# Layer 0 of a four-layer image model: causal mask moved to VectorE, a 64-channel remainder computed by halves, decays spread by DMA

## The chip, the cores and the metric

The kernel is one program on one core of a Trainium2 chip. A core has a matrix engine (TensorE, PE in the profile, with its weight loads shown apart as PEld), a vector engine (VectorE, DVE), an activation engine (ScalarE, ACT), a general engine (GpSimd, POOL) and a queue engine (SyncE, SP) that issues most of the DMA transfers. Each engine executes its own list of instructions in order and waits on semaphores for the others. The metric is the device time of one launch in microseconds (us), lower is better. Before the change it is 15763.65 us, the median of three runs that lie between 15760.87 and 15764.36.

## The reference, cut to what matters

Four layers follow each other, each of the form x = x + layer(group_norm(x)), on 16 images of 192 channels of 32 x 32 pixels. Only layer 0 is touched. For each image it computes, with L = 1024 tokens (the pixels in order), 12 heads of 32 channels and an inner width of 384:

```python
h = _layernorm(seq, ln_w, ln_b)
x_in, z = jnp.split(h @ w_up + b_up, 2, axis=-1)
x_act = silu(causal_conv4(x_in))
q, k, v = x_act @ w_q, x_act @ w_k, x_in
i_pre, f_pre = gin @ w_i + b_i, gin @ w_f + b_f      # gin = concat(q, k, v)
# for each token: log_f = log_sigmoid(f);  m_new = max(log_f + m, i)
#   C = exp(log_f + m - m_new) * C + exp(i - m_new) * v k^T       (n likewise, with k)
#   h = C q / max(|n . q|, 1)
hn = per_head_norm(hs) * mh_w + mh_b
x1 = seq + ((hn + skip * x_act) * silu(z)) @ w_down + b_down      # 384 -> 192
y = conv3x3(x1 + silu(seq @ w_lin + b_lin)) + conv2_b             # then batch norm over all images
```

The recurrence over tokens is the part that the change is about. The batch norm at the end needs statistics over all 16 images, so the convolution's output goes to DRAM and is normalised by the code of the later layers.

## The kernel before, in words

`layer0` (lines 153 to 722) first loads the weights, and then loops over the 16 images with a hardware loop (`tc.For_i` on line 386). All instructions of one image are the loop's body. At its end the engines meet: each of them waits for the last work of every engine and for every DMA semaphore before it jumps back to the loop's start.

The recurrence is computed in 8 chunks of 128 tokens. Inside a chunk it is a product of matrices: for each head a 128 x 128 matrix of decays D, where D[s, t] = exp(a_t + (i_s - F_s)) for s up to t and zero for s after t, is multiplied by the scores k_s . q_t. Across chunks a state C (`cst`) and a normaliser n (`nst`) are carried, and q is scaled by a decay from the chunk's start (`isc`) before it meets them; the scaled q is `qs`.

The steps that the text follows are these.

- *Gates.* The gate values live with the heads on the partitions: `isc`, `wks`, `at`, `it` and their like (lines 430 to 485).
- *q's decays.* `qs` (lines 528 to 536): for each half of the tokens and each group g of four heads, a matmul with the constant `sel` spreads the four decays to 128 partitions in a PSUM bank, and VectorE multiplies q by them. That is 6 matmuls and 6 products for each image.
- *Scores.* `scores(n)`, n = 0 to 11 (lines 588 to 609), handles two (chunk, head group) pairs. It owns four PSUM banks S[0] to S[3], one for each head of the group. Columns 0 to 255 of a bank take the exponents of D, columns 256 to 511 the products of k and q. First four bfloat16 matmuls put the mask (0 or -1e30) into the four banks (line 595), then 16 matmuls add the exponents and 16 the products (line 600). ScalarE takes the exponential of the first half into an SBUF tile `d` (line 606), VectorE multiplies it by the second half (line 609).
- *A chunk's preparation and end.* `turned(c)` (lines 565 to 586) transposes v and k, and `finish(c)` (lines 611 to 678) multiplies D by v, adds the state's part, updates the state on VectorE and GpSimd, and normalises: ScalarE takes a square, TensorE a mean (lines 667 and 669), ScalarE a logarithm and an exponential (lines 670 and 671), VectorE the product and the affine part (lines 672 and 674), GpSimd the gate (line 678).
- *Fill.* `conv3(b)` (from line 348) is the 3 x 3 convolution of the image before, written as a generator: `fill(k)` issues its next k matmuls where TensorE would else wait. It reads `ypad`, the padded sum of the two branches of the image before. Channels 128 to 191 of `ypad` are held twice, on partitions 0 to 63 and, one column to the left, on partitions 64 to 127, so that one matmul covers two taps.
- *The order.* From `scores(0)` to the last `finish` the order is the program's own (`tc.manual_schedule()`); around it a scheduler orders the instructions. In that part the sequence for n = 0 to 11 is: scores, perhaps `turned`, and then either `finish` of a chunk (n = 2, 3, 5, 6, 8, 9, 11) or a fill of three matmuls (n = 0, 1, 4, 7, 10).
- *The two projections.* Lines 699 to 719 compute silu of the linear branch and the down projection for two groups of output channels, e = 0 (channels 0 to 127) and e = 1 (channels 128 to 191, twice side by side, so that the weights are 256 columns wide), for two halves hf of the tokens: 8 matmuls with `w_lin`, 12 with `w_down`, and six writes to `ypad` by VectorE on line 716. The sum with the input needs the normalised input on other partitions; four DMAs copy it to `xr`.

In all of this each float32 matmul is seen twice in the trace, as two passes.

Of the kernel before, what the change touches and what calls it, by code (L numbers as in the profile page):

```python
# [11 lines left out]
F32 = mybir.dt.float32  # L12
BF16 = mybir.dt.bfloat16
AF = mybir.ActivationFunctionType
ALU = mybir.AluOpType
AX = mybir.AxisListType
PSUM = bass.MemoryType.PSUM
DRAM = bass.MemoryType.DRAM

C, H, W = 192, 32, 32  # L20
L = H * W
HL = L // 2
P6 = 96
INNER, NH, DH = 384, 12, 32
CH = 128
# [6 lines left out]
def half(hf):  # L32
    return slice(hf * HL, (hf + 1) * HL)


def matmuls(nc, out, pairs):
    n = len(pairs)
    for i, (l, r) in enumerate(pairs):
        nc.tensor.matmul(out, lhsT=l, rhs=r, start=(i == 0), stop=(i == n - 1))
# [107 lines left out]
def rows(ap):  # L147

    return ap.rearrange("p (h w) -> p h w", w=W)
# [3 lines left out]
def layer0(tc, cx, NB, ydram, sdram):  # L153
    nc, I = cx.nc, cx.I
    with ExitStack() as ctx:
        wp = ctx.enter_context(tc.tile_pool(name="a_w", bufs=1))
        psp = ctx.enter_context(tc.tile_pool(name="a_ps", bufs=2, space=PSUM))
        pss = ctx.enter_context(tc.tile_pool(name="a_pss", bufs=1, space=PSUM))
        psn = ctx.enter_context(tc.tile_pool(name="a_psn", bufs=1, space=PSUM))
# [4 lines left out]
        def ps():  # L164

            turn[0] = (turn[0] + 1) % 6
            if turn[0] < 4:
                return pss.tile([128, HL], F32, tag="s%d" % turn[0], name="ps")
            return psp.tile([128, HL], F32, tag="ps", name="ps")
# [15 lines left out]

        w_down = wp.tile([128, 3, 256], F32, name="w_down")
        w_lin = wp.tile([P6, 2, 256], F32, name="w_lin")
        for t, nm, p in ((w_down, "w_down", 128), (w_lin, "w_lin", P6)):  # L190
            nc.sync.dma_start(t[:, :, 0:C], I[nm].rearrange("(k p) o -> p k o", p=p))
            nc.sync.dma_start(t[:, :, C:], I[nm][:, 128:C].rearrange("(k p) o -> p k o", p=p))
        w_c2 = wp.tile([128, 9, C], F32, name="w_c2")
        nc.sync.dma_start(w_c2, I["conv2_wT"][0:128])
        w_c2p = wp.tile([128, 2, 3, C], F32, name="w_c2p")
        for u in range(2):
            r = slice(64 * u, 64 * u + 64)
# [16 lines left out]
        b_down, b_lin, c2_b = vec3("b_down"), vec3("b_lin"), vec3("conv2_b")  # L214
# [12 lines left out]
        b_i, b_f = b_if  # L227
        conv_k = wp.tile([128, 3, 4], F32, name="conv_k")
        nc.sync.dma_start(conv_k, I["conv_k"].rearrange("(k p) t -> p k t", p=128))
        mask = wp.tile([128, 2 * CH], BF16, name="mask")  # L230
        identb = wp.tile([128, 128], BF16, name="identb")
        hmask = wp.tile([128, 4 * HW1], F32, name="hmask")
        nc.sync.dma_start(hmask, I["c_hmask"])
        nc.vector.tensor_copy(identb, cx.ident)

        blocks = wp.tile([128, 4, DH], F32, name="blocks")
        nc.vector.tensor_copy(blocks, hmask.rearrange("p (j d) -> p j d", d=HW1)[:, :, 0:DH])
# [18 lines left out]
        for u in range(2):  # L256
            for g in range(3):
                o = NH * u + 4 * g
# [33 lines left out]
        with tc.tile_pool(name="a_pre", bufs=1) as pre:  # L292
            m32 = pre.tile([128, CH], F32, name="m32")
            nc.sync.dma_start(m32, I["c_causal"])
            nc.vector.tensor_copy(
                mask.rearrange("p (i t) -> p i t", i=2),
                m32.unsqueeze(1).to_broadcast([128, 2, CH]),
# [88 lines left out]
        with tc.For_i(0, NB, 1) as b:  # L386
# [87 lines left out]
            isc = gp.tile([128, NCH, CH], F32, tag="e1", name="isc")  # L474
            nc.vector.tensor_add(isc, at3, mprev.unsqueeze(2).to_broadcast([128, NCH, CH]))
            nc.scalar.activation(isc, isc, AF.Exp)
            wks = gp.tile([128, NCH, CH], F32, tag="lf", name="wks")
            al = sm.tile([128, NCH], F32, tag="al", name="al")
            nc.vector.tensor_copy(al, at3[:, :, CH - 1])
# [40 lines left out]
            for c0 in range(0, NCH, 4):  # L520
# [3 lines left out]
                nc.vector.tensor_copy(  # L524
                    gtok[:, c0 : c0 + 4], p.rearrange("p (c r) -> p c r", c=4)[:, :, 0:NH]
                )

            qs = big.tile([128, 3, L], F32, tag="h", name="qs")
            for hf in range(2):
                for g in range(3):  # L530
                    p, r = ps(), slice(32 * g, 32 * g + 32)
                    nc.tensor.matmul(
                        p, lhsT=sel[r, g, :], rhs=isc.rearrange("p c t -> p (c t)")[r, half(hf)],
                        start=True, stop=True,
                    )
                    nc.vector.tensor_mul(qs[:, g, half(hf)], qT[:, g, half(hf)], p)

            for g in range(3):
                nc.scalar.activation(
# [48 lines left out]
            def scores(n):  # L588


                todo = [divmod(2 * n + i, 3) for i in range(2)]
                S = [pss.tile([128, HL], F32, tag="s%d" % j, name="s") for j in range(4)]
                two = slice(0, 2 * CH)
                for j in range(4):
                    nc.tensor.matmul(S[j][:, two], lhsT=identb, rhs=mask, start=True, stop=False)
                for l_, r_, o in ((itg, at, 0), (kT, qT, 2)):
                    for i, (c, g) in enumerate(todo):
                        cs = slice(c * CH, (c + 1) * CH)
                        for j, r in enumerate(blocks4):
                            nc.tensor.matmul(  # L600
                                S[j][:, (o + i) * CH : (o + i + 1) * CH], lhsT=l_[r, g, cs],
                                rhs=r_[r, cs] if o == 0 else r_[r, g, cs], start=False, stop=(o == 2 and i == 1),
                            )
                for j in range(4):
                    d = wk2.tile([128, 2 * CH], F32, tag="D", name="D", bufs=12)
                    nc.scalar.activation(d, S[j][:, two], AF.Exp)  # L606
                    for i, (c, g) in enumerate(todo):
                        D[c, g, j] = d[:, i * CH : (i + 1) * CH]
                    nc.vector.tensor_mul(d, d, S[j][:, 2 * CH :])  # L609

            def finish(c):

# [83 lines left out]
                pass  # L696


            xr = big.tile([128, 2, L], F32, tag="qT", name="xr")
            for r, e, q, a in (  # L700
                (slice(0, P6), 0, slice(0, P6), 0), (slice(P6, 128), 0, slice(0, 32), 1),
                (slice(0, 64), 1, slice(32, P6), 1), (slice(64, 128), 1, slice(32, P6), 1),
            ):
                nc.sync.dma_start(xr[r, e, :], xn[q, a, :])
            for e in range(2):
                for hf in range(2):
                    o = slice(e * 128, (e + 1) * 128)
                    pl = ps()
                    matmuls(nc, pl, [(w_lin[:, i, o], xn[:, i, half(hf)]) for i in range(2)])
                    lin = wk2.tile([128, HL], F32, tag="lin", name="lin")  # L710
                    nc.scalar.activation(lin, pl, AF.Silu, bias=b_lin[:, e : e + 1])
                    pd = ps()
                    matmuls(nc, pd, [(w_down[:, g, o], hT[:, g, half(hf)]) for g in range(3)])
                    nc.vector.tensor_add(lin, lin, xr[:, e, half(hf)])
                    for r, x in ((slice(0, 128), 1),) if e == 0 else ((slice(0, 64), 1), (slice(64, 128), 0)):
                        nc.vector.scalar_tensor_tensor(
                            ypad[r, e, 1 + 16 * hf : 17 + 16 * hf, x : x + W], rows(pd[r, :]),
                            b_down[r, e : e + 1], rows(lin[r, :]), op0=ALU.add, op1=ALU.add,
                        )

        for _ in conv3(NB - 1):
            pass
# [1245 lines left out]
```

## Time and profile before

| what | value |
|---|---|
| median of the runs | 15763.65 us |
| the profiled execution's own time | 15761.82 us |
| its span on the core | 15760.0 us |
| TensorE busy over the span | 12662.9 us (80%) |
| VectorE busy over the span | 12218.0 us (78%) |
| TensorE busy from 400 to 800 us, in layer 0 | 384.80 of 400 us |
| VectorE busy in the same stretch | 176.95 of 400 us |
| granted TensorE clock in the same stretch | 0.99 of full |
| restart of layer 0's loop on TensorE, two neighbours | 2477.89 and 2679.24 us |

The profiled execution took 1.82 us more than its span, and 1.83 us less than the median. Layer 0 lasts from the start to some 3328 us, where the last matmul of its convolution ends; one image takes a little over 201 us. A row of the profile names the line, the engine, the operation and the tiles; `busy` is the time in which an engine executes, and a releaser is what ended the idle time before. A busy TensorE is no TensorE at its peak, because matmuls overlap: their starts tell more than their durations.

### The profile page before, as it was taken

The page shows a single profiled execution, that of the slowest core. Times are in us where ns is not written, and L with a number is a line of the kernel's source. Part 1 is how long each engine was busy: PE and PEld are TensorE (multiplying, and loading weights), DVE is VectorE, ACT ScalarE, POOL GpSimd, SP SyncE. Part 2 cuts the span into 40 slices and gives each one's busy share as a digit, 9 for nine tenths or more (in the row PEclk, how much of TensorE's full clock was granted, in tenths as well). Part 3 has the DMA queues.
Part 4 walks back from the last instruction along what each step waited for, and adds up shares of the span by engine and source line. Part 5 has one row for each costly group of instructions (what it writes and reads, how often), then busy time and mean ns, then how long its engine had stood idle before and what let it go on. Part 6 is the DMA issues. An engine that isn't in the chain of part 4 may idle for free. (4 is left out here: it accounts for less than half of the span.)

```text
span 15760.0 us, 197355 instructions
## 1 busy us (share of the span) xinstructions
PE 12662.9 (80%) x72684; PEld 5062.6 (32%) x72684; DVE 12218.0 (78%) x10138; ACT 9273.8 (59%) x12098; POOL 9921.9 (63%) x5837
## 2 busy tenths in 40 slices
PE   8999999987777878778777777777787777878755
PEld 4555555542222222222222222222222222222212
DVE  4444444416898989989888898988989898988995
ACT  3333333325666666666666666666666666666664
POOL 0000000005687878787878787878878787878886
PEclk9999999998787878878788888888888887878766
DMA  1000000016787877778787878787877777777774
GB/s 26 15 15 15 15 14 15 15 47 168 193 202 196 198 199 192 207 185 209 180 209 182 210 186 209 185 210 186 204 193 196 194 200 192 198 201 188 203 181 114
DMA packets 858797, 2421.52 MB, mean 154 GB/s; under 512 B 117952, under 2 KB 237840, under 8 KB 850192
## 3 DMA queue, kind: packets, MB, share of 16 engines
q1 hardware_dynamic: 848592, 2407.09, 59.7%
q8 instruction: 583, 9.55, 0.3%
q10 hardware_dynamic: 9280, 2.08, 0.1%
q14 instruction: 342, 2.80, 0.1%
HBM read 2025.36 MB, written 366.67 MB: 152 GB/s over the span
## 5 line engine op out<-in xcount | busy, mean ns | idle before, releaser
L1829 POOL TENSOR_TENSOR hc<-h,cb 128x1024 f32<-128x1024 f32 x3072 | 7245.4, 2371 | 2057.6 <-DVE h L1817 1546.5
L1817 DVE TENSOR_TENSOR_SCAN h<-dA,xt 128x1024 f32<-128x1024 f32 x3072 | 6914.9, 2273 | 303.6 <-POOL hc L1829 295.9
L1808 DVE TENSOR_TENSOR xt<-xt,bb 128x1024 f32<-128x1024 f32 x3072 | 3632.9, 1227 | 929.7 <-ACT xt L1797 800.6
L1801 ACT ACTIVATE dA<-dl,A 128x1024 f32<-128x1024 f32 x3072 | 3506.3, 1146 | 778.6 <-DMA dl<-dld 670.2
L1859 PE MATMUL acc<-hc,sel 128*32 128x256 f32 x24576 | 2399.7, 471 | 1756.8 <-POOL hc L1829 1753.8
L766 PE MATMUL mm<-pad,dg 96*96 96x512 f32 (+1 forms) x5760 | 2964.3, 650 | 14.4 <-ACT pad L766 11.0
L1797 ACT COPY xt<-du 128x1024 f32<-128x1024 f32 x1536 | 1557.7, 1014 | 1387.9 <-DVE h L1817 1216.3
L1859 PEld LDWEIGHTS acc<-hc,sel 128*32 128x32 f32 x24576 | 560.6, 120 | 4094.9 <-POOL hc L1829 2956.9
L766 PEld LDWEIGHTS mm<-pad,dg 96*96 96x96 f32 (+1 forms) x5760 | 1022.0, 191 | 1517.1 <-issue 1400.8
L583 POOL TENSOR_TENSOR vw<-va,gtok 128x396 f32<-128x396 f32 x112 | 95.3, 851 | 1707.1 <-ACT va L575 1707.1
L766 PE MATMUL mm<-x,wgt 96*128 96x512 f32 (+1 forms) x1664 | 1055.2, 770 | 114.9 <-ACT z L766 42.8
L766 POOL TENSOR_TENSOR t<-x 96x512 f32<-96x512 f32 (+7 forms) x544 | 689.6, 1290 | 212.5 <-PE mm L766 199.9
L1850 PE MATMUL acc<-y,ident 128*128 128x512 f32 x576 | 444.1, 863 | 452.1 <-ACT y L1869 451.4
L678 POOL TENSOR_TENSOR x_in<-x_in,sz 128x384 f32<-128x384 f32 x128 | 116.8, 913 | 749.8 <-DVE x_in L674 674.0
L766 POOL TENSOR_TENSOR dlh<-dlh,e 128x512 f32<-128x512 f32 x384 | 488.6, 1272 | 157.4 <-ACT e L766 151.4
L766 PE MATMUL mm<-d,xT 128*96 128x256 f32 x2048 | 562.3, 412 | 19.2 <-ACT o L766 17.4
L766 POOL TENSOR_TENSOR duh<-dlh,xx 128x512 f32<-128x512 f32 x384 | 537.4, 1399 | 30.2
L766 PE MATMUL mm<-xd,dtw 12*128 12x512 f32 x768 | 532.8, 779 | 14.1 <-ACT dlh L766 14.1
L766 PEld LDWEIGHTS mm<-x,wgt 96*128 96x128 f32 (+1 forms) x1664 | 338.1, 223 | 633.5 <-issue 360.9
L374 PE MATMUL pc<-ypad,w_c 128*128 128x512 f32 (+1 forms) x1224 | 468.3, 631 | 89.3 <-PEq L386 46.1
L609 DVE TENSOR_TENSOR D<-D,s 128x256 f32<-128x256 f32 x768 | 271.0, 415 | 325.9 <-ACT D L606 325.9
L606 ACT ACTIVATE D<-s 128x256 f32<-128x256 f32 x768 | 232.7, 390 | 430.6 <-PE s L600 430.6
(314 smaller groups left out, 15277.6 us busy)
## 6 DMA issues: line engine op xcount, KB each, us to landing
dl<-dld SPq DMA_DIRECT2D x1536, 512.0 KB
du<-dud SPq DMA_DIRECT2D x1536, 512.0 KB
dld<-dlh SPq DMA_DIRECT2D x384, 256.0 KB
dud<-duh SPq DMA_DIRECT2D x384, 256.0 KB
bb<-xdr SPq DMA_DIRECT2D x128, 512.0 KB
cb<-xdr SPq DMA_DIRECT2D x128, 512.0 KB
dg<-dqd SPq DMA_DIRECT2D x288, 192.0 KB
xxd<-xg SPq DMA_DIRECT2D x16, 1536.0 KB
```

Of the source, the lines that this page charges most:

```text
L374: nc.tensor.matmul(p[r, :], lhsT=w_, rhs=v, start=(n == 0), stop=(n == 14))
L606: nc.scalar.activation(d, S[j][:, two], AF.Exp)
L609: nc.vector.tensor_mul(d, d, S[j][:, 2 * CH :])
L678: nc.gpsimd.tensor_mul(hT[:, :, cs], hT[:, :, cs], sz[:, :, cs])
L766: return f(out, *args, **kw)
L1797: self.nc.scalar.copy(self.xt[n], self.du[n])
L1801: self.nc.scalar.activation(self.dA[u % 3], self.dl[n % 2], AF.Exp, scale=self.A[:, blk, n : n + 1])
L1808: self.nc.vector.tensor_mul(self.xt[(n + 1 + blk) % 2], self.xt[n % 2], self.bb[blk])
L1817: nc.vector.tensor_tensor_scan(*views, 0.0, op0=ALU.mult, op1=ALU.add)
L1829: self.nc.gpsimd.tensor_mul(*views)
L1850: nc.tensor.matmul(acc, lhsT=self.cx.ident, rhs=self.y[:, g, half(pair)], start=True, stop=False)
L1859: nc.tensor.matmul(self.acc[rows4(q), q4(s)], lhsT=self.sel[:, m, :], rhs=self.hc[u % 3][:, q4(q)], start=False, stop=(s + m + blk == 3),)
```

## The change

Three parts of layer 0 are computed in other ways. What follows after the loop stays as it was, instruction for instruction, on every engine.

First, the mask. The four mask matmuls at the start of `scores` go away, and with them the bfloat16 identity. The first exponent matmul into each bank now starts the bank. The exponential of a masked entry can then be large, so VectorE limits D to 2 as it multiplies by the scores, and a second VectorE product multiplies by a mask of ones and zeros. The pool of `d` tiles grows from 12 to 14.

Second, q's decays. `isc` is written to DRAM, read back with each row repeated over 32 partitions by three DMAs, and multiplied by q with three GpSimd products. The six matmuls and six VectorE products go away.

Third, the projections. Channels 128 to 191 are computed once, with the two halves of the tokens side by side: partitions 0 to 63 take half 0, partitions 64 to 127 half 1. That makes three output tiles in place of four; the third has ten matmuls of 64 output rows. Two DMAs inside SBUF then copy each half of these channels to where the convolution's second copy lies. The weights lose their doubled columns and two load DMAs.

```diff
-            nc.sync.dma_start(t[:, :, 0:C], I[nm].rearrange("(k p) o -> p k o", p=p))
-            nc.sync.dma_start(t[:, :, C:], I[nm][:, 128:C].rearrange("(k p) o -> p k o", p=p))
+            nc.sync.dma_start(t, I[nm].rearrange("(k p) o -> p k o", p=p))
...
+            nc.vector.tensor_scalar(m32, m32, -1.0, 1.0, op0=ALU.max, op1=ALU.add)
...
             nc.scalar.activation(isc, isc, AF.Exp)
+            nc.sync.dma_start(iscd, isc[0:NH].rearrange("p c t -> p (c t)"))
+            qs = big.tile([128, 3, L], F32, tag="h", name="qs")
+            for g in range(3):
+                nc.sync.dma_start(
+                    qs[:, g, :], iscd[4 * g : 4 * g + 4].unsqueeze(1).to_broadcast([4, DH, L])
+                )
...
-            qs = big.tile([128, 3, L], F32, tag="h", name="qs")
-            for hf in range(2):
-                for g in range(3):
-                    p, r = ps(), slice(32 * g, 32 * g + 32)
-                    nc.tensor.matmul(
-                        p, lhsT=sel[r, g, :], rhs=isc.rearrange("p c t -> p (c t)")[r, half(hf)],
-                        start=True, stop=True,
-                    )
-                    nc.vector.tensor_mul(qs[:, g, half(hf)], qT[:, g, half(hf)], p)
+            for g in range(3):
+                nc.gpsimd.tensor_mul(qs[:, g, :], qs[:, g, :], qT[:, g, :])
...
-                for j in range(4):
-                    nc.tensor.matmul(S[j][:, two], lhsT=identb, rhs=mask, start=True, stop=False)
...
-                                rhs=r_[r, cs] if o == 0 else r_[r, g, cs], start=False, stop=(o == 2 and i == 1),
+                                rhs=r_[r, cs] if o == 0 else r_[r, g, cs],
+                                start=(o == 0 and i == 0), stop=(o == 2 and i == 1),
...
-                    d = wk2.tile([128, 2 * CH], F32, tag="D", name="D", bufs=12)
+                    d = wk2.tile([128, 2 * CH], F32, tag="D", name="D", bufs=14)
...
-                    nc.vector.tensor_mul(d, d, S[j][:, 2 * CH :])
+                    nc.vector.scalar_tensor_tensor(
+                        d, d, 2.0, S[j][:, 2 * CH :], op0=ALU.min, op1=ALU.mult
+                    )
+                    nc.vector.tensor_mul(d, d, mask)
...
-            for e in range(2):
-                for hf in range(2):
-                    o = slice(e * 128, (e + 1) * 128)
-                    pl = ps()
-                    matmuls(nc, pl, [(w_lin[:, i, o], xn[:, i, half(hf)]) for i in range(2)])
-                    lin = wk2.tile([128, HL], F32, tag="lin", name="lin")
-                    nc.scalar.activation(lin, pl, AF.Silu, bias=b_lin[:, e : e + 1])
-                    pd = ps()
-                    matmuls(nc, pd, [(w_down[:, g, o], hT[:, g, half(hf)]) for g in range(3)])
...
+            for n in range(3):
+                e = n // 2
+                parts = [(n, slice(0, 128), slice(0, 128))] if n < 2 else [
+                    (0, slice(128, C), lower), (1, slice(128, C), upper)
+                ]
+                pl, pd = ps(), ps()
+                for p, w_, v, k in ((pl, w_lin, xn, 2), (pd, w_down, hT, 3)):
+                    for i in range(k):
+                        for hf, o, r in parts:
+                            nc.tensor.matmul(
+                                p[r, :], lhsT=w_[:, i, o], rhs=v[:, i, half(hf)], start=(i == 0), stop=(i == k - 1)
+                            )
...
+            nc.sync.dma_start(ypad[upper, 1, 1:17, 0:W], ypad[lower, 1, 1:17, 1 : 1 + W])
+            nc.sync.dma_start(ypad[lower, 1, 17:33, 1 : 1 + W], ypad[upper, 1, 17:33, 0:W])
```

In the new order of instructions the DMAs of the decays stand on SP's queue after the load of the next image and ahead of the convolution's stores; the three GpSimd products are that engine's first work in an image; and the two copies inside SBUF are the last entries of SP's queue before the loop's end. On TensorE the projections come as: `w_lin` of tile 0, the last `finish`, `w_lin` of tiles 1 and 2, the first `w_down` matmul of tile 2, then `w_down` of tile 0, tile 1, and the other five of tile 2.

## The prediction

> **What bounds the kernel now.** I first read the stretches of layer 0, which lasts some 3.3 ms of 15.8; the rest is left as it was, instruction for instruction. The columns are length and busy time of PE, PEld, DVE, ACT and POOL.
>
> ```profile
> core 0: us, PE busy (x) PEld busy (x) DVE busy (x) ACT busy (x) POOL busy (x), PEclk, DMA share, GB/s
> 464.00:665.40 201.40, 193.80 (x1812) 105.52 (x1812) 88.76 (x179) 78.11 (x150) 18.20 (x30) 0.99 0.05 14
> ```
>
> One image: TensorE works 193.8 of 201.4 us, VectorE 88.8, GpSimd 18, the DMA engines 5%. So TensorE sets the pace, and work moved to the others is free unless it makes TensorE wait. Who waits for whom on TensorE over layer 0 (us in total, times, longest) says where the other 7.6 us go:
>
> ```profile
> PE pc L374 <- PEq L386: 46.1, 15, 3.2
> PE pc L374 <- ACT yo L377: 39.0, 32, 1.4
> PE s L595 <- DVE qs L536: 15.8, 48, 0.3
> PE ps L39 <- POOL x_in L678: 13.5, 16, 1.0
> ```
>
> 3.1 us an image at the loop's end (L386), 2.4 for the convolution's bank, 1.0 where the first mask matmuls wait for the qs products, 0.8 for the last chunk. Then the timeline of TensorE before the first scores:
>
> ```profile
> 2559.06 1.99 PE L532 MATMUL ps<-isc,sel 32*128 32x512 f32 x12
> 2560.98 1.12 PE L374 MATMUL pc<-ypad,w_c2p 64*128 64x512 f32 x2
> 2562.16 0.27 PE L595 MATMUL s<-mask,identb 128*128 128x256 bf16 x1
> 2562.75 0.27 PE L595 MATMUL s<-mask,identb 128*128 128x256 bf16 x1 [0.33 <-DVE qs L536]
> ...
> 2564.15 0.73 PE L600 MATMUL s<-at,itg 32*128 32x128 f32 x16
> ```
>
> and an ordinary step, where four masks take 0.53 us from start to start (2570.62 to 2571.15):
>
> ```profile
> 2570.62 0.60 PE L595 MATMUL s<-mask,identb 128*128 128x256 bf16 x4
> 2571.15 0.73 PE L600 MATMUL s<-at,itg 32*128 32x128 f32 x16
> ```
>
> Last the loop's end, VectorE's last write and TensorE's restart, and then the stretches before and after the restart, where the first number after POOL's is the granted clock:
>
> ```profile
> 2676.23 1.51 DVE L716 SCALAR_TENSOR_TENSOR ypad<-ps,v_b_down,lin 64x512 f32<-64x512 f32 x2 [1.23 <-PE ps L39]
> 2679.24 3.57 PE L374 MATMUL pc<-ypad,w_c 128*128 128x512 f32 x4 [3.05 <-PEq L386]
> ```
>
> ```profile
> 2676.00:2679.20 3.20, 0.19 (x1) 0.00 (x0) 1.62 (x3) 0.16 (x1) 0.00 (x0) 0.98 0.00 0
> 2679.20:2682.60 3.40, 3.35 (x4) 1.45 (x5) 2.63 (x7) 1.12 (x1) 0.00 (x0) 0.51 0.00 0
> ```
>
> The restart comes 1.50 us after VectorE's end at 2677.74, and the next 3.4 us run at clock 0.51.
>
> [...] restarts at 464.07 and 2880.61 lie 12 images apart, 201.38 us each, which is 59.0 such windows. [...] here the small store to `sdram`, issued at 2658.46, released ScalarE at 2660.60, 2.14 us. [...] no row of layer 0 shows pieces of 128 B.
>
> **The change, for one image; 16 of them.**
>
> *Masks, n = 1 to 11.* Eleven times 0.53 us go, some 0.1 of each perhaps needed again for the switch of tile shape: 11 x 0.50 = -5.5.
>
> *The start.* From 2559.06 to 2564.15 are 5.09 us; only the convolution's 1.1 stays: -4.0. Nothing else is late there: the last copy of k (L499) ended at 2558.52, and scores(0) would start near 2560.2.
>
> *Decays by DMA.* `isc` is ready at 2743.26 in the next image, 20.5 us ahead of its first scores. The store takes some 2.4 us, the reads 1.5 MB: the 768 KB of the next image kept the engines 47% busy for 6 us, 2.8 us of full work, so 5.6 here plus 2.4 of latency. They land near 2754. SP has no store to make between (the next is at 2767). GpSimd's three products at 2.37 us (the 128x1024 row of line 1829) are in order with q's last copy at 2756.8 and end by 2762; `vw`, queued behind them, is wanted at 2763 or later, and `qs` itself only by the second `finish`, over 20 us later. Cost 0; without that cover the products' 7 us would be seen. The six VectorE products (3.7 us) were hidden but for the wait counted above.
>
> *The VectorE products.* A bank is now released after a limited product from PSUM (0.415 us, as L609) and, for all but the first, the pairs before it. [...] a pair about 0.80 with the overlap of neighbours. 48 x 0.42 = 20 us more for VectorE, which had over 110 idle. But where a `finish` comes right before, VectorE starts D late: in step n = 4 TensorE ends the norm's matmuls at P = 2591.51, and D starts at 2594.23, P + 2.72. The fourth bank comes free at P + 2.72 + 3 x 0.80 + 0.42 = P + 5.54. Without masks TensorE wants it at P + 1.10 (scores) + 1.10 (turned) + 2.87 (fill) + 0.1 = P + 5.17: a wait of 0.4. Step 7 is like it; step 10, with a shorter `turned` (5.22 from mask to mask before, 4.69 now), waits 0.75. In the other steps D starts 1.6 after scores and the bank is free by 4.4, wanted at 4.8 or later; D itself is read a step later. Sum +1.5, from 0 (if the pair costs 0.65) to +3.
>
> *Projections.* Eight passes fewer at full width, but the last chunk's values come at 2670.77 by the chain through ScalarE (with four table loads), VectorE and GpSimd, which doesn't move. Behind them stood 12 passes of 0.43; now 6 of 0.43 and at most 10 of 0.23 (the convolution's 64-row form does 12 in 2.73): 4.9 for 5.2, -0.3. What is saved ahead of 2670.77 becomes idle time, 3.6 to 4.2 us, and may halve the clock for the passes behind: 0 to +1.7, taken as +0.5.
>
> *The copies inside SBUF.* They are issued after VectorE's last writes, and every engine waits for their semaphores at the loop's end; nothing hides them. A copy has 64 x 16 pieces of 128 B, 64 for each of 16 engines. From issue to landing a store of 64 rows took 2.4 us (the two stores of `yo`: 2658.88, the second held until 2661.26). For pieces I have the three 4-byte loads of `tq` after layer 0: 3456 pieces, about 2.9 us of DMA work on 16 engines, 14 ns a piece, so 0.9 us. Together +3.3. Low end +2.1 (the small store); high end, at four times the price of a piece (64 x 0.056 + 2.4 = 6.0) and with a part of the first copy still in line, +7.
>
> *Start of the launch.* Two loads fewer on SP, which idles from 3.84 to 6.66 behind one of them: 0 to -4 once, taken as -2.
>
> Sum: -5.5 - 4.0 + 1.5 - 0.3 + 0.5 + 3.3 = -4.5 us an image, 196.9, which is 57.7 clock windows. The loop restarts in step with these windows, because a restart that comes late in one has less slow time ahead of it. The nearest whole number is 58, 197.97 us, and I take that: -3.4 x 16 - 2 = -57 us. In the profiled execution 15760.0 + 1.8 - 57 = 15705; the median is 1.8 above that execution, so 15707, taken as 15705.
>
> **The rivals.**
>
> *Ledger without the lock* (0.28): -4.5 x 16 - 2 gives 15690; with the low ends of waits, clock and copies -7.7 x 16 - 2, 15639.
>
> *Gain swallowed* (0.15): waits for the fourth bank at their high end and the copies at +5, -1.3 an image, or a lock at 59 windows: 15740 to 15764. For it: both unknown costs lie on the path. Against: it needs both.
>
> *Copies as a bottleneck* (0.09), slower: [...] The sum turns at +7.8 for the loop's end, and passes +0.2% at +9.8: with 128 pieces on each engine in line and 2.4 us of latency, that is 58 ns a piece, four times my figure. At 100 ns it is +15.2, giving 15880. Against: the 4-byte loads.
>
> *Decays late* (under 0.03): the second `finish` would wait for `qs`; needs a delay of over 20 us.
>
> **How the numbers follow.** Likeliest, 58 windows or near it: 0.45, its own range 15690 to 15725. With the rivals 0.28, 0.15, 0.09 and 0.03 the range 15640 to 15770 leaves out some 0.17. About 0.2% (32 us) is what a measurement of this kernel can tell from no change; faster by more: 0.76, within: 0.15, slower: 0.09.
>
> **What would show it.** Lines 595 and 532 are gone; scores(0) starts 5 us sooner after the `wks` transposes; short waits of TensorE on the D rows in steps 4, 7 and 10; TensorE's gap at the loop's end grows from 3.1 to some 6 us, with a DMA as releaser; the restart's period is near 198. I am wrong if the copies land over 8 us after VectorE's end, if D's waits appear in every step, or if the layers after layer 0 change by more than 20 us.

## The result: no gain, and the profile after

The changed kernel takes 15772.4 us (median of 20 runs) against 15763.1 for the kernel before: a ratio of 1.0004, 95% interval 0.9998 to 1.0010. The forecast was 15705. The 57 us expected are not there.

All three parts did what they say, and the work did leave TensorE. The stretches of one image of layer 0 in the changed kernel (length, busy time of PE, PEld, DVE, ACT and POOL, granted clock, DMA share, GB/s):

```profile
core 0: us, PE busy (x) PEld busy (x) DVE busy (x) ACT busy (x) POOL busy (x), PEclk, DMA share, GB/s
461.10:662.50 201.40, 187.34 (x1752) 100.98 (x1752) 109.19 (x218) 77.40 (x149) 26.82 (x33) 0.97 0.08 22
```

TensorE is busy for 187.3 us instead of 193.8, VectorE for 109.2 instead of 88.8, and the image still takes 201.4. The saved time has turned into waiting and slow clock. Who TensorE waits for over layer 0 (us in total, times, longest):

```profile
PE pc L375 <- PEq L387: 100.4, 15, 6.9
PE ps L718 <- POOL x_in L681: 62.5, 16, 4.0
PE pc L375 <- ACT yo L378: 40.1, 33, 1.4
PE s L598 <- DVE D L609: 14.8, 48, 0.3
```

The loop's end went from 46.1 to 100.4 us and the wait for the last chunk of `hT` from 13.5 to 62.5. The convolution's wait (40.1) is the old one, and the last line stands where the wait for `qs` stood.

An image can be cut at three points of TensorE's timeline: its first exponent matmul (`scores(0)`), the end of the last norm matmul (the `dsel` row of the last `finish`), and its last row. In us, for the image that restarts at 2477.89 before and at 2475.32 after:

```
                                        before   after   difference
restart to scores(0)                     86.26   82.49     -3.77
scores(0) to the last norm matmul        95.48   93.79     -1.69
last norm matmul to TensorE's last row   16.56   18.37     +1.81
TensorE's last row to the restart         3.05    6.63     +3.58
sum                                     201.35  201.28     -0.07
```

The first piece went as forecast. On TensorE's timeline `scores(0)` follows the `wks` transposes and the convolution's one row, with no broadcast products and no masks between:

```profile
2555.74 1.09 PE L531 MATMUL ps<-ident,wks 128*128 128x128 f32 x8
2556.76 1.12 PE L375 MATMUL pc<-ypad,w_c2p 64*128 64x512 f32 x2
2557.81 0.73 PE L598 MATMUL s<-at,itg 32*128 32x128 f32 x16
```

The second piece lost most of its gain behind steps 4, 7 and 10: VectorE's products of these steps hold the banks that the scores of steps 5, 8 and 11 want. The products of step 4 and the scores of step 5, from the same timeline, rows of TensorE, VectorE and GpSimd (start, duration):

```profile
2589.02 0.78 PE L598 MATMUL s<-at,itg 32*128 32x128 f32 x6
2590.11 0.59 PE L598 MATMUL s<-at,itg 32*128 32x128 f32 x9 [0.31 <-DVE D L609]
...
2590.55 0.71 PE L598 MATMUL s<-qT,kT 32*128 32x128 f32 x13
2591.19 0.86 PE L622 MATMUL nd<-D,va 128*32 128x128 f32 x24
...
2586.58 0.41 DVE L609 SCALAR_TENSOR_TENSOR D<-D,s 128x256 f32<-128x256 f32 x1
2587.03 0.91 DVE L612 TENSOR_TENSOR D<-D,mask 128x256 f32<-128x256 f32 x1
2587.86 0.41 DVE L609 SCALAR_TENSOR_TENSOR D<-D,s 128x256 f32<-128x256 f32 x1
2588.30 0.62 DVE L612 TENSOR_TENSOR D<-D,mask 128x256 f32<-128x256 f32 x1
...
2589.64 0.41 DVE L609 SCALAR_TENSOR_TENSOR D<-D,s 128x256 f32<-128x256 f32 x1
...
2586.76 0.91 POOL L681 TENSOR_TENSOR x_in<-x_in,sz 128x384 f32<-128x384 f32 x1 [4.04 <-DVE x_in L677]
2587.62 1.03 POOL L583 TENSOR_TENSOR vw<-va,gtok 128x396 f32<-128x396 f32 x1
```

The scores of step 5 take from 2589.02 to 2591.19, 2.17 us, where an undisturbed step takes 1.1. So the step loses 1.07 us, of which the list above counts only the 0.31 of idle time. The fourth bank comes free only after the last limited product (L609, end 2590.05), and three mask products (L612) stand ahead of it. The first two of these ran beside products of two inputs on GpSimd and took 0.91 and 0.62 us. Over all of layer 0, the 462 mask products that overlap no GpSimd instruction take 0.42 to 0.43 us; the median is 0.63 for the 128 that overlap L583 alone, and 0.92 for the 96 that overlap L681.

The third piece, the tail. First the windows around the last chunk's arrival, then TensorE's timeline:

```profile
2659.30:2662.70 3.40, 0.00 (x0) 0.00 (x0) 2.83 (x7) 2.83 (x4) 0.90 (x1) 1.00 0.00 0
2662.70:2666.10 3.40, 3.39 (x5) 1.50 (x6) 0.50 (x1) 0.00 (x0) 0.00 (x0) 0.61 0.02 5
2666.10:2669.60 3.50, 3.50 (x12) 0.75 (x10) 0.75 (x1) 0.00 (x0) 0.00 (x0) 0.90 0.00 0
```

```profile
2655.02 3.80 PE L718 MATMUL ps<-x_in,w_down 128*64 128x512 f32 x8
2662.71 7.26 PE L718 MATMUL ps<-x_in,w_down 128*128 128x512 f32 x16 [3.89 <-POOL x_in L681]
2676.60 2.05 PE L375 MATMUL pc<-ypad,w_c 128*128 128x512 f32 x2 [6.63 <-PEq L387]
```

TensorE stands idle for 3.89 us, and the 16 passes behind the wait run at clock 0.61 and 0.90. They take 7.26 us from the first start to the last end; the same 16 passes take 5.46 at full clock, in the run below that moves the Silu rows. The clock's record has one stretch of half clock here, 3.41 us long, from 0.71 us after their start. The fourth piece is the gap of 6.63 us in the last row. VectorE had its last write at 2671.54; the restart is 5.06 us later, where it was 1.50.

### The profile page after: what moved, and what is told of

Same layout as the page of the kernel before. It is cut to its first block, busy times and chain, and to the rows that moved or that the text cites. A ratio compares the mean times of both kernels' runs of the same rounds, so it can differ in the third digit from the quotient of the medians.

```text
span 15778.2 us, 196250 instructions
## 1 busy us (share of the span) xinstructions
PE 12591.2 (80%) x71724; PEld 4999.5 (32%) x71724; DVE 12539.0 (79%) x10762; ACT 9264.7 (59%) x12082; POOL 10055.9 (64%) x5885
## 5 line engine op out<-in xcount | busy, mean ns | idle before, releaser
L536 POOL TENSOR_TENSOR qs<-qs,qT 128x1024 f32<-128x1024 f32 x48 | 112.9, 2353 | 1534.3 <-DMA qs<-iscd 1518.4
L779 POOL TENSOR_TENSOR t<-x 96x512 f32<-96x512 f32 (+7 forms) x544 | 689.3, 1288 | 228.5 <-PE mm L779 208.7
L375 PE MATMUL pc<-ypad,w_c 128*128 128x512 f32 (+1 forms) x1224 | 471.0, 633 | 147.1 <-PEq L387 100.4
L681 POOL TENSOR_TENSOR x_in<-x_in,sz 128x384 f32<-128x384 f32 x128 | 116.7, 912 | 692.4 <-DVE x_in L677 692.4
L612 DVE TENSOR_TENSOR D<-D,mask 128x256 f32<-128x256 f32 x768 | 427.4, 556 | 26.3
```

The source lines that it names most:

```text
L375: nc.tensor.matmul(p[r, :], lhsT=w_, rhs=v, start=(n == 0), stop=(n == 14))
L612: nc.vector.tensor_mul(d, d, mask)
L681: nc.gpsimd.tensor_mul(hT[:, :, cs], hT[:, :, cs], sz[:, :, cs])
L779: return f(out, *args, **kw)
```

## The experiments

Theory A is the table: terms that add up, with three sinks (bank waits, the idle tail with its slow clock, the copies at the loop's end). Theory B, a rival, is that the period can only be a whole number of clock windows of 3.413 us, so that a gain below the next step is lost whatever it came from; both kernels have periods of 59.0 such windows. The windows are read from the clock's record in the two profiles: the 17 stretches of half clock up to 3300 us before, and the 32 after, are all 3.413 or 6.827 us long, and within a profile start whole multiples of 3.4133 us apart, to within 0.002. Theory C is, in each run, that the suspected cause isn't one. Times given as differences are the ratio, less one, times 15763. Periods are the mean distance of restarts of the loop in the profile.

**The third part alone.** The kernel before, with the loads and the projections of the changed one.

> The kernel before with the projections' part of the change alone (last 64 channels by halves side by side, two copies inside SBUF at the loop's end, two loads fewer); masks and decays as before. Theory A (the ledger with the terms as the trace of after shows them: loop end +3.6 us, cold clock in the passes behind the last chunk about +1.8): the loop's period grows from 201.4 to 206 to 207 us, total about +80 us over before, near 15845. Theory B (the period keeps to whole clock windows of 3.413 us): 204.8 or 208.2 us, +55 or +109 us. Theory C (this part costs next to nothing, the gain was lost elsewhere): period 201.4 to 202, total within 15 us of before.

Ratio 1.0083 (1.0070 to 1.0097), +131 us; periods mostly 208.2, mean 208.7. C falls: this part costs 7 us an image. Against before the tail grew by 2.81 us and the gap at the loop's end by 3.75. A was 2 us too low: the 16 passes behind the last chunk took some 8.2 us here and not 7.26, with half clock for 6.83 us and not 3.41. B's 208.2, or 61 windows, is met by twelve images of fourteen (207.9 to 208.3). The other two last 212.0 and 212.1; in each the clock is at half for 10.24 us more, about the start of the second piece.

**The other two parts without the third.** The changed kernel with the loads and projections of before, `D` in 13 buffers.

> The changed kernel with the projections of before (full width, no copies inside SBUF): masks as a product and decays by DMA alone; 13 buffers for D in place of 14, for room. Theory A: start -3.8 and masks with their waits -1.7 us an image, so a period of about 196 us and -85 us against before, near 15678. Theory B (whole windows): 197.9 us (58 windows, -55 us) or 194.5 (57, -109 us). Theory C (the gain is lost in the bank waits and not at the loop's end): period 201 and no gain.

Ratio 0.9949 (0.9935 to 0.9962), -80 us; mean period 195.86. A's sum is met. B as it is stated is not: single periods lie between 194.9 and 196.9, 57.1 to 57.7 windows.

**The decays alone**, in the kernel before: `iscd`, the store, the three loads and the GpSimd products replace the matmuls of L532 and the products of L536.

> The kernel before with the decays' part alone (decays by DMA, product with q on GpSimd; masks and projections as before). Only three of six broadcast products of TensorE a head group go, so the first mask matmuls stay. Theory A (removed work comes off the path): 2.0 to 2.4 us off before the first scores, no wait for qs; period 199.0 to 199.5, or less by up to 1.6 if restarts come warm. Theory B (whole windows): 201.4 (no gain) or 198.0. Theory C (the DMA part makes something late): slower than before.

Ratio 0.9968 (0.9956 to 0.9980), -50 us; period 197.93. The expectation counted the removed matmuls wrongly (all six go), so the gain that A names, 2.0 to 2.4 us, was too small: the first piece shrinks by 3.4, from 86.26 to 82.87, of which the matmuls are 1.99 and the wait for `qs` 1.0. A's period holds only with its allowance for warmer restarts, and 197.93 is also B's 198.0, so this run doesn't tell the two apart. Nothing came late.

**The masks alone**, in the kernel before, `D` in 13 buffers.

> The kernel before with the masks' part alone (product on VectorE; decays and projections as before; 13 buffers for D). Theory A: 5.8 us of mask matmuls in 11 steps and some 2 in the first step go, bank waits of 3.4 us and about 0.7 of switching come: -3 to -4 us an image, period 197.5 to 198.5. Theory B (whole windows): 198.0 or 201.4. Theory C (VectorE's extra work delays more than the banks): no gain, 201.

Ratio 0.9989 (0.9981 to 0.9997), -17 us; mean period 200.4. Nearer to C than to A. TensorE's timeline at the first scores shows why:

```profile
2550.16 2.39 PE L598 MATMUL s<-at,itg 32*128 32x128 f32 x15
2552.29 0.28 PE L598 MATMUL s<-qT,kT 32*128 32x128 f32 x3
```

Fifteen passes take 2.39 us where 16 take 0.73 in the full change: VectorE's six `qs` products, still there, end at 2551.90, and the scores take over their PSUM banks. In the kernel before, the masks' matmuls stood in this place and did the waiting (the 0.33 us for `qs` at 2562.75). Then TensorE waits another 1.2 us for `yo`, and in ten images of fourteen the clock is at half for 3.4 or 6.8 us about here; in this image the next six passes take 5.05 us and not 2.84, at clock 0.50. So the masks' part gains more beside the decays' part: alone they shorten the period by 1.0 and 3.4 us, together by 5.5.

**The order of VectorE's products.** In the changed kernel:

```diff
-                    nc.vector.tensor_mul(d, d, mask)
+                    ds.append(d)
+                for d in ds:
+                    nc.vector.tensor_mul(d, d, mask)
```

> The changed kernel with another order on VectorE: the four limited products of a step first, which free the four banks, and then the four mask products. Nothing is left out. Theory A: the waits for banks in steps 4, 7 and 10 (3.4 us an image) go almost whole, period 198.0 to 198.5 us, -45 to -55 us against after, near 15720. Theory B (whole windows): 198.0 us, or no change at all if the 3.4 us are not quite saved. Theory C (the waits in these steps come from something other than the mask product ahead of the bank's release): waits and time stay as in after.

Ratio 0.9971 (0.9961 to 0.9981), -46 us against before; period 197.96. The wait for banks is gone from the list, and the second piece is 90.36 us instead of 93.79. The scores of step 5 and the products of step 4 in this kernel, TensorE and then VectorE:

```profile
2546.94 0.73 PE L598 MATMUL s<-at,itg 32*128 32x128 f32 x16
2547.49 0.60 PE L598 MATMUL s<-qT,kT 32*128 32x128 f32 x13
...
2544.50 1.40 DVE L610 SCALAR_TENSOR_TENSOR D<-D,s 128x256 f32<-128x256 f32 x4
2545.82 1.85 DVE L615 TENSOR_TENSOR D<-D,mask 128x256 f32<-128x256 f32 x4
```

All four banks are free at 2545.9, before TensorE wants the first. The mask products' place ahead of the banks' release is shown as the cause of the waits, 3.43 us an image. As 3.43 us is also one window to within 0.02, the run says nothing on B.

**Half a window more work.** In the changed kernel four matmuls of zeros are added to the sums of the first scores step:

```diff
+                    for j in range(4 if n == 0 and o == 2 else 0):
+                        nc.tensor.matmul(
+                            S[j][:, two], lhsT=w_c2[:, j, 0:128],
+                            rhs=zero.to_broadcast([128, 2 * CH]), start=False, stop=False,
+                        )
```

> The changed kernel with four more matmuls of 128x256 (two passes each, with a moving operand of zeros, so the sums are unchanged) in the first scores step of each image, where TensorE never waits: 1.7 us an image, half a clock window. Theory A (no lock): period 203.1 us, +27 us against after, near 15800. Theory B (the period keeps to whole windows): 201.4 and no change, or 204.8 and +55 us.

Ratio 1.0046 (1.0032 to 1.0059), +72 us against before, +66 against the changed kernel; period 204.82, that is 60.0 windows. The added passes take 2.01 us, and the period grew by 3.40. So B holds here. In the mean over the images the second piece, which holds the added passes, grew by 2.1. The rest is slow clock: the passes behind the last chunk took 8.34 us and not 7.26, with half clock for two windows (6.83 us) and not one, and the restart's piece and the gap grew by 0.2 together.

**Without the copies.** The two DMAs inside SBUF are removed, which leaves that part of the work out.

> The changed kernel without the two copies inside SBUF at the loop's end, so one row of the last 64 channels' halves lacks in ypad: this leaves out part of the work. Theory A (the copies cost what the trace shows between VectorE's end and the restart, 3.6 us): period 197.8 us, -57 us against after. Theory B (whole windows): 58 windows, 198.0 us, -55 us, or 57 (194.6) if a shorter gap at the loop's end also leaves less slow time. Theory C (the barrier at the loop's end costs this in any case, copies or not): no change.

Ratio 0.9961 (0.9947 to 0.9974), -61 us against before; mean period 197.90. TensorE's last row to the restart is 3.06 us, as before the change. C falls: it is the copies and not the barrier, 3.57 us an image. The rounding is loose: three periods of 197.4 and one of 199.5, in turn, make 232 windows in four images.

**Both good parts, with the order.** The second run's kernel with the reordered products.

> Masks and decays of the change, projections of before, and the four limited products of a step ahead of the four mask products. Nothing is left out. Theory A (costs simply add): the run without the reordering had a mean period of 195.85 us; less the bank waits of 3.4 us gives 192.4, -145 us against before, near 15615. Theory B (whole windows when the slow clock after the restart can take up the difference): without slow clock the period would be some 191.5 us, 56.1 windows; it is 56 windows (191.2), 57 (194.6), or swings between images as without the reordering, where some restarts came warm. Theory C (nothing more to be had): as without the reordering, 15680.

Ratio 0.9904 (0.9889 to 0.9919), -151 us. Mean period 191.9, single ones 191.6 and 192.4: A's 192.4 and 15615 against 15617.6 measured. It is not a whole number of windows (56.2), though B had named such swings between images as a third way. The second piece is 90.36 again.

**Its tail by hand, and with the clock kept up.** Two kernels made from the last one: one with the order of the projections written out, and one that adds two matmuls of zeros at the end of an image:

```diff
+                fl = ps()
+                for i, w in enumerate((HL, 128)):
+                    nc.tensor.matmul(
+                        fl[:, 0:w], lhsT=w_c2[:, i, 0:128], rhs=zero.to_broadcast([128, w]),
+                        start=(i == 0), stop=(i == 1),
+                    )
+                nc.scalar.copy(zero, fl[:, 0:1])
```

> As the run before it in this list, with the tail written out by hand: all four w_lin products, then the w_down products of both tiles of the first half, then of the second half with the single write of the first 128 channels last; ScalarE's Silu rows come after the last finish and not between its Ln and Exp. Nothing is left out. Theory A (TensorE bounds the tail): its gap of 0.8 us before the last chunk goes, and one write of 0.6 us less stands behind its last row: -1.4 us an image, about -22 us. Theory B: a whole window or none, -55 us or 0. Theory C: the chain through ScalarE does not bound this tail and no gain appears.

> As the run before it in this list, with two matmuls more at the end of an image (128x512 and 128x128 on a moving operand of zeros, 1.1 us, result copied on ScalarE into the zero it came from), so that TensorE idles about 2 us and not 3 at the loop's end. Theory A (the slow clock after the restart is only a cost): the restart comes warm in more images, -1.0 to -1.6 us an image, -16 to -26 us. Theory B (the slow clock is also what holds the period at whole windows): the period is no longer a whole number of windows and takes the value without slow clock, near 190 us. Theory C (2 us of idle time are enough to halve the clock): no change, or +0.3 us an image if the copy comes after VectorE's end.

0.9926 (0.9912 to 0.9939) and 0.9916 (0.9902 to 0.9931); mean periods 193.40 and 193.35. The first is a miss: the Silu rows still stood between Ln and Exp on ScalarE, and the `w_lin` pair that used to run ahead of the last `finish` was now behind it, so TensorE waited 28.1 us in all for `h` there (2.5 in the changed kernel). The second missed A's gain of 1.0 to 1.6 us and B's period near 190, and is what its theory C had allowed for. But it shows what the slow clock does. All its restarts come at full clock (four passes in 1.96 us, where those of before take 3.57), and its 14 periods lie between 193.34 and 193.39, 56.65 windows. Without the fill they swung from 192.97 to 193.72. So in these two kernels the slow time after a restart is what moves the period about, and where it is gone the period is constant and on no whole window. There was no gain: the restart's piece shrank by 0.41 us, and the last two pieces grew by 0.36, since the fill's copy on ScalarE ended 0.5 us after VectorE and held up the barrier.

**Silu behind the last finish.** In the changed kernel the tail is written out with TensorE's rows in the same order, and ScalarE's Silu rows after Ln and Exp (`lin_mm` and `down_mm` issue the matmuls of a tile; `last` is the list of those of the 64-row tile):

```diff
+                lin_mm(0)
                 finish(ready)
...
+                for n in range(3):
+                    if n:
+                        lin_mm(n)
...
+                    nc.scalar.activation(lin, pls[n], AF.Silu, bias=b_lin[:, e : e + 1])
...
+                down_mm(2, last[:1])
+                down_mm(0, [(i, tiles[0][1][0]) for i in range(3)])
+                down_mm(1, [(i, tiles[1][1][0]) for i in range(3)])
+                down_mm(2, last[1:])
```

> The changed kernel with its tail written out: TensorE's rows in the same order as in the changed kernel, but ScalarE's three Silu rows behind the last finish's Ln and Exp and not between them. Nothing is left out. Theory A (the last chunk of hT comes late by the Silu rows and their table loads, TensorE idles 3.9 us for it and then runs its passes at half clock): hT's last chunk some 5 us sooner, no gap, passes at full clock; TensorE's tail ends about 12.4 us after the norm's matmuls and not 18.5, period near 195.3 us (up to 1.7 more or 2 less, by how much slow clock the restart then has), about -97 us against after, near 15675. Theory C (the chain is bound by something else, the stores to DRAM that ScalarE issues): the wait and the period stay within 1 us of after.

Ratio 0.9938 (0.9925 to 0.9952), -98 us against before; mean period 195.70. First ScalarE's timeline in the changed kernel:

```profile
2652.55 1.28 ACT L722 ACT_TABLE_LOAD   x1 [1.69 <-DMA sdram<-st]
...
2653.84 0.69 ACT L722 ACTIVATE lin<-ps,v_b_lin 128x512 f32<-128x512 f32 x1
2654.55 1.28 ACT L673 ACT_TABLE_LOAD   x1
2655.84 0.49 ACT L673 ACTIVATE h<-ps 128x384 f32<-128x384 f32 x1
2656.35 1.28 ACT L722 ACT_TABLE_LOAD   x1
2657.64 0.69 ACT L722 ACTIVATE lin<-ps,v_b_lin 128x512 f32<-128x512 f32 x1
2658.35 1.28 ACT L674 ACT_TABLE_LOAD   x1
2659.64 0.52 ACT L674 ACTIVATE h<-h 128x384 f32<-128x384 f32 x1
```

and then, in the experiment, ScalarE and TensorE:

```profile
2583.66 0.49 ACT L673 ACTIVATE h<-ps 128x384 f32<-128x384 f32 x1 [3.44 <-DMA sdram<-st]
2584.18 0.52 ACT L674 ACTIVATE h<-h 128x384 f32<-128x384 f32 x1
2584.72 1.28 ACT L735 ACT_TABLE_LOAD   x1
2586.01 1.85 ACT L735 ACTIVATE lin<-ps,v_b_lin 128x512 f32<-128x512 f32 x3
...
2580.80 3.75 PE L705 MATMUL ps<-xn,w_lin 96*128 96x512 f32 x12
2584.38 9.09 PE L711 MATMUL ps<-x_in,w_down 128*64 128x512 f32 x24
```

Exp ended 8.7 us after TensorE had turned to `w_lin` in the first kernel (2651.44 to 2660.16), and ends 3.9 us after it in the second (2580.80 to 2584.70). TensorE no longer waits, its 24 passes take 9.09 us in one piece, and the third piece is 12.51 us instead of 18.37: 3.9 us of idle time and 1.8 of slow clock are gone. C falls: the chain was made long by Silu rows and table loads. With TensorE never waiting, this tail is also 4 us shorter than the old one (16.56). How much of that belongs to the third part of the change is open, since no run moves the Silu rows with the projections of before; the one by hand above meant to, and didn't.

**All of it.** That kernel with the reordered products, the 64-row tile of `w_down` before the last 128-row one, and the copies issued right behind that tile's writes:

```diff
-                down_mm(1, [(i, tiles[1][1][0]) for i in range(3)])
                 down_mm(2, last[1:])
+                down_mm(1, [(i, tiles[1][1][0]) for i in range(3)])
```

> The run before it in this list, with the limited products ahead of the mask products, and with the 64-row tile of w_down ahead of the last 128-row one, so that its copies inside SBUF are issued while TensorE still works. Nothing is left out. Theory A (terms add): -3.4 us for the bank waits and -2.6 for the copies' issue 2.6 us sooner against TensorE's end: period 189.3 us (188 to 191), -190 us against before, near 15575. Theory B (whole windows): 187.7 (55) or 191.2 (56). Theory C (copies cannot be hidden, since the loop's end waits for them however early they are): 192.

Ratio 0.9885 (0.9870 to 0.9900), -181 us: faster than either kernel. Mean period 189.43, alternating between 188.9 and 189.9: A's 189.3, and neither of B's values. The pieces of one image are 82.1, 90.3, 12.7 and 3.9. VectorE's and TensorE's timelines at its end:

```profile
2514.39 1.53 DVE L750 SCALAR_TENSOR_TENSOR ypad<-ps,v_b_down,lin 64x512 f32<-64x512 f32 x2 [0.90 <-PE ps L714]
2517.16 0.75 DVE L750 SCALAR_TENSOR_TENSOR ypad<-ps,v_b_down,lin 128x512 f32<-128x512 f32 x1 [1.24 <-PE ps L714]
...
2520.96 1.19 PE L375 MATMUL pc<-ypad,w_c 128*128 128x512 f32 x1 [3.84 <-PEq L387]
```

The copies' source is written by 2515.92, and the restart comes 5.04 us later, as in the changed kernel (5.06). Only now TensorE works for 1.2 us of that time and VectorE for 2.0, and the gap is 3.84 and not 6.63.

## The prediction, point by point

**What bounds the kernel** was right: every piece above is set by TensorE and by what it waits for.

**The start (-4.0):** -3.77. Right, and nothing else was late there.

**Decays at no cost:** right in the sum, wrong on the way. The loads did not take 5.6 us in all but 5 us each. The windows between their landings show the DMA engines at a quarter:

```profile
2544.50:2549.30 4.80, 4.80 (x12) 2.09 (x11) 0.00 (x0) 1.18 (x2) 0.00 (x0) 1.00 0.26 105
2549.30:2554.30 5.00, 5.00 (x13) 2.28 (x12) 0.00 (x0) 2.12 (x3) 2.35 (x2) 1.00 0.26 105
```

The last landed at 2559.3 and its product started then, 1.5 us after `scores(0)` and not ahead of it. The 20 us of cover until the second `finish` absorbed that.

**Masks (-5.5):** right for the matmuls. With the bank waits removed, the piece from `scores(0)` on is 5.12 us shorter. Eleven times 0.53 would be 5.83. The 0.1 set aside for a switch of tile shape was the author's estimate: in the trace of before the masks of a step start 0.109 us apart, and the first exponent matmul, on 32 rows and not 128, starts 0.203 us after the last of them (2570.948 to 2571.151). What of the 0.71 us between 5.83 and 5.12 is such a switch was not measured.

**The VectorE products (+1.5, range 0 to +3): failed.** It was 3.43. The 0.42 us taken for a mask product held where GpSimd was idle (the 462 above). The step took a pair at 0.80 us everywhere. In steps 4, 7 and 10, the only ones that matter, GpSimd multiplies at the same moment. In step 4 the first two pairs took 1.28 and 0.99 us (2586.58 to 2587.86 to 2588.85), in step 7 likewise; in step 10 only the first was stretched. With the pairs as measured, the step's own sum gives the fourth bank free at P + 6.1 and not P + 5.5, where TensorE wants it at P + 5.2: a wait of 0.9 us and not 0.4, near the 1.07 that was measured (2.17 less 1.10). The place (the products of steps 4, 7 and 10, fourth bank) was right. That GpSimd causes the stretch is read from the coincidence in the trace: without a GpSimd product of two tensors beside it, no mask product of layer 0 takes over 0.51 us. But no run took GpSimd's products away.

**Projections (-0.3, clock +0.5, range to +1.7): failed.** The tail cost +1.81. The idle time was 3.89 us as forecast, and the chain that "doesn't move" didn't move. The clock term was mis-sized: the passes lost 1.80 us (7.26 for 5.46), where 0.5 was taken and 1.7 was the end of its range. The saving of 0.3 us behind the chunk wasn't there either: the old 12 passes take 5.42 us from first start to last end, the new 16 at full clock 5.46. (The step's 4.9 is right as the time from the first start to the last one.) The step also took the chain as given, and asked only what it does to TensorE. The Silu rows in it were in the trace of before, ScalarE's timeline:

```profile
2663.89 0.49 ACT L670 ACTIVATE h<-ps 128x384 f32<-128x384 f32 x1
2664.40 1.28 ACT L711 ACT_TABLE_LOAD   x1
2665.70 0.69 ACT L711 ACTIVATE lin<-ps,v_b_lin 128x512 f32<-128x512 f32 x1
2666.40 1.28 ACT L671 ACT_TABLE_LOAD   x1
2667.70 0.52 ACT L671 ACTIVATE h<-h 128x384 f32<-128x384 f32 x1
```

They were worth 6 us once TensorE had less to do.

**Copies (+3.3):** +3.57 by the run without them. The term and its working hold: the 2080 packets at that place kept the engines busy for 23.9% of 7 us on 16 engines, 12.9 ns a packet for an assumed 14. The latencies it works with, 2.14 and 2.4 us, are measured on stores to DRAM in the trace of before, the first of them issued by ScalarE.

**The sum, taken to 58 windows: failed with its terms.** With the sizes measured it is -3.8 - 1.7 + 1.8 + 3.6 = -0.1, and 201.3 is 59 windows. That 5.5 us of gain met 5.4 of loss, and left a time so near the old one, is chance.

The lock itself is half true. The grid of 3.413 us is there (in the clock's record, as told with theory B), and a restart that comes later in a slow stretch does have less of it ahead. From the second restart on, those of before come 0.11 to 0.24 us after the start of a stretch, with 3.31 to 3.17 us of half clock to go; those of the changed kernel come 2.63 to 3.13 us after it, with 4.19 to 3.69 to go. A period that is a whole number of windows, image by image, was found where every restart comes slow in the same way (59.0, 59.0, 58.0, 58.0, 60.0, and 61.0 in twelve images of fourteen), and there 2.0 us of extra work became a whole window. In the other eight kernels most single periods were not whole. But the grid comes back over a few images where the slow stretches differ from one restart to the next: two images of the last experiment make 111.0 windows, three of the one before it 172.0, three with the tail by hand 170.0, four without the copies 232.0, and the first images with two parts of the change come in pairs of 115.0. Only with the fill, where no restart is slow, is there no such number: two to five images make 113.29, 169.93, 226.58 and 283.22 windows, the same to 0.02 all along. So the lock is one of a pattern of images, and taking one image's sum to the nearest window was no rule to rely on.

How long TensorE must idle for half clock to come is not shown by these runs. It came with the gaps of 3.05 to 3.17 us at all fifteen restarts of before, and with one of 2.30 with the tail by hand, where the first four passes took 2.99 us and not 1.96; but the same 3.06 us in the kernel with masks and decays alone was followed by none at four restarts of fifteen. After the 1.60 us with the fill it never came.

**The rivals.** "Gain swallowed" (0.15) is what happened, and in part by its own mechanism, the waits for the bank at (in fact over) their high end; the 59 windows that it names as another way are there too. Its second term was off: the copies cost 3.6 and not 5, and the slow clock made up the difference. "Copies as a bottleneck", whose dear pieces were an assumption that no trace had shown, and "decays late" did not occur. The result lies at the range's upper end, 15770: the new median is 15772.4, and the old one times the ratio 15770.0.

**The launch (-2):** can't be seen. From the fifteenth restart to the end the profiled runs of all these kernels differ by up to 60 us (12650 to 12710), with the same instructions but for one image. For the same reason the layers after layer 0 (+20 us in the one profile of after) tell nothing.

## What to carry to other kernels

Work taken off the bounding engine pays only up to the next wait, so ask for each wait that it moves towards which rows stand in that chain, and whether they need to: here two Silu rows with their table loads, one ahead of Ln and one between Ln and Exp, were worth 6 us an image, more than any part of the change. On the engine that gets the work, put first what releases a buffer, and price it as it runs beside its neighbours, not alone. A DMA as the last thing in a loop was paid in full here, 3.57 us; issued 2.0 us before the end of VectorE's last write it was half hidden, with 3.05 us from that write to the restart where it was 5.06 with the copies last and 1.50 before the change.

## What was not expected of the hardware

A float32 product on VectorE that takes 0.42 us mostly took 0.62 to 0.99 beside products of two inputs on GpSimd, and once an image 2.0 to 2.5 beside the 128x1024 one. The limited product, with one input in PSUM, stayed at 0.41 in the same places.

A load with four rows of a DRAM tensor spread over 32 partitions each (512 KB) moved 105 GB/s at a mean DMA share of 0.26, 5 us.

After 3.9 us of idle time TensorE lost 1.8 to 2.9 us in 16 passes (7.26 to 8.34 for 5.46). In the changed kernel one stretch of half clock, 3.41 us long, began 0.5 to 1.0 us after their start; in two of the experiments it was 6.83 us long. A restart of the loop cost TensorE between 0 and 2.6 us of slow clock: with masks and decays changed, the first piece is 81.6 us where no window is slow, and up to 84.2.
